# Two-layer cross-attention on one core: last key block padded to 65 rows, first products of the first projection in one piece, result transposes in eights, weights' sums moved

## The chip, the cores and the metric

The kernel runs on one core of one Trainium2 chip. The metric is the device time of one execution in microseconds; lower is better. A core has TensorE (PE in the profile, its weight loads PEld), VectorE (DVE), ScalarE (ACT), GpSimd (POOL) and SyncE (SP), which run side by side and wait for each other at semaphores. Everything is in float32.

## What is computed

Eight batches of 100 query rows (width 1024) attend to 1444 key rows (width 512) twice, with different weights. The first layer adds its projected output to the queries; the second adds its values and normalises. Cut to what matters:

```python
def layer0(query, key, Wq, bq, Wk, bk, Wv, bv, Wo, bo):
    Q, K, V = query @ Wq + bq, key @ Wk + bk, key @ Wv + bv
    weights = softmax(Q @ K.T * 1024 ** -0.5, axis=-1)
    return query + (weights @ V) @ Wo + bo

def layer1(emb, latent, Wq, bq, Wk, bk, Wv, bv, gamma, beta):
    q, k, v = emb @ Wq + bq, latent @ Wk + bk, latent @ Wv + bv
    w = softmax(q @ k.T / sqrt(1024), axis=1)      # over the 100 query rows
    x = w @ v + emb
    return (x - mean(x)) * rsqrt(var(x) + 1e-6) * gamma + beta

x = layer0(x, ctx, ...)       # x: 8 x 100 x 1024, ctx: 8 x 1444 x 512
x = layer1(x, ctx, ...)
```

## The kernel before

**Algebra.** The kernel never builds K or V. It multiplies the weights first (`weight_products`), so that scores are `g @ ctx.T` with g of width 512 per query, and it sums the rows of ctx with the attention weights (`A`, 512 wide) before it projects. Large products are cut in quarters and done with seven products instead of eight, with sums on VectorE (`seven_products`, `inner_product`, `project0`). In these a stationary tile has 128 rows and 128 columns.

**The loop of a batch.** `alternated` runs 48 steps for a batch b: 12 key blocks m times 4 column chunks k. A step gives two matmuls to `weighted_rows` (line 914, the tile A; each has 64 weight columns and goes to one half of the output's partitions) and two to the scores of batch b + 2 (`scores`, line 938, in layer 0; `scores_by_keys`, line 978, in layer 1, the tile s), which also have 64 columns or fewer. In the trace each of these matmuls is two records. In the last two batches of a layer there are no further scores, and A stands alone.

**Rows of A's matmuls.** In layer 0 a key block has 120 rows (124 in the last). In layer 1 a block has 128, and the last has the rest, 1444 - 11 * 128 = 36 (`keys`). The weights of a batch, `w`, have a buffer of 12 blocks of 100 columns, in three rotating buffers; `softmax1` fills the first 36 rows of the last block. `load_rows` brings ctx in four quarters of three blocks, `load_features` its transpose in four chunks; both go through SP's queue into ten rotating buffers (tag "unit"), so that a load is issued when an earlier buffer comes free.

**The first projection.** `project0` (line 1070) is a generator. Its first yield hands out another one, `first`, with eight matmuls of width 400: the products X and Z of one half, for the queries of batches 0 to 3. Its second yield hands out an inner product of seven matmuls of width 200 (tiles o_z_x, o_z_z and so on, called with ahead=True: the sums S1, T1, S3, T3, T2, S2, T4, S4 are given to VectorE first). The caller (lines 1364 to 1379) runs one matmul of `first` after every fourth step of batch 6, and one of the inner product after every fourth step of batch 7; three steps of `queries1`, which give VectorE sums of weights, also go into batch 7. The rest of `project0` follows batch 7.

**The end of a batch in layer 1.** `finish` (line 1271) transposes the 100 finished query rows back with eight matmuls of 100 columns against the identity (line 1249), four for each half, with one step of the loop between the halves. VectorE adds the value bias times the sum of the weights (`r`, line 1253) and forms the statistics; POOL takes the power -1/2, ACT scales, and POOL adds the result to the output by a DMA. The table `finished` says at which step of which batch the seven first batches are finished; batch 7 is finished at the end by `untransposed` and `project_last`.

**The sums of the weights.** `weight_sums` (line 1182, POOL) adds the blocks of `w` to `wsum`, of which there are three buffers. `weight_totals` (line 1198) transposes the wsum of two batches on TensorE and sums them on VectorE to `r`. It is called at step 27 of batches 1, 3 and 5 and at step 8 of batch 7.

**Order.** TensorE's instructions keep the order in which the program gives them (`manual_schedule`). VectorE calls made while `in_order` is set keep theirs; other engines' instructions are placed by the framework's scheduler. PSUM has six banks in the pool "ps" and two in "ps2". After batches 3 and 6 of layer 1 `project1` projects the batches since the last one, and gives VectorE the rest of the softmax of batch 5 or 7 between its products.

## Time and profile before

| what | us |
|---|---|
| median of 3 runs (617.16 to 619.68) | 617.25 |
| profiled execution, its own time | 619.34 |
| its span, first to last instruction | 617.6 |
| PE busy | 604.3 |
| DVE busy | 419.2 |
| ACT busy | 164.8 |
| POOL busy | 100.5 |
| A, 3072 matmul records (line 921), busy | 241.0 |
| s of layer 1, 1472 records (line 990), busy | 116.8 |
| s of layer 0, 1120 records (line 951), busy | 125.5 |
| layer 0, batches 0 to 5 (203.2 to 316.2) | 113.0 |
| layer 0, batches 6 and 7 (316.2 to 345.9) | 29.7 |
| layer 1, batches 0 to 3 (430.8 to 502.4) | 71.6 |
| layer 1, batches 4 and 5 (521.8 to 563.2) | 41.4 |
| layer 1, from batch 7 to the end (586.4 to 617.6) | 31.2 |

The granted clock of TensorE was 0.998 of full speed over the span. Busy times of one engine count overlapping instructions once. The times in brackets are places in the trace, counted from its first instruction; the rows of the loop are read from the first and last records of A. Records of A and s overlap[...]: where both run, one starts 0.043 us after the other in the mean, though each lasts 0.25. So a record's duration says little about its cost, and the distance between starts says it.

### The profile page before, as it was taken

The numbers are of one execution on the slowest core, as the hardware profiler recorded it, in microseconds if no ns is written. First come the engines' busy times: TensorE is split into PE (matmuls) and PEld (weight loads), VectorE is DVE, ScalarE is ACT, GpSimd is POOL, SyncE is SP. The second block draws the span as 40 slices with busy tenths as digits, with TensorE's granted clock in tenths as the row PEclk, the third lists the DMA queues.
The fourth block names the chain that finished last, engine by engine and source line by source line (L and its number), as shares of the span: only waits on it lengthen the run. The fifth ranks groups of instructions, "written<-read, shape, count | busy, mean of one in ns | idle before, by whom it ended". The sixth has DMA issues, their size and how long they took to land.

```text
span 617.6 us, 16433 instructions
## 1 busy us (share of the span) xinstructions
PE 604.3 (98%) x7088; PEld 504.4 (82%) x7088; DVE 419.2 (68%) x915; ACT 164.8 (27%) x374; POOL 100.5 (16%) x141
## 2 busy tenths in 40 slices
PE   9999999999999999998999999999999999999985
PEld 8886467688995999998987666788999999998972
DVE  2986789797793798776559587857423346743785
ACT  1322223314503344323330001103323311134313
POOL 3110111212230000000000001206522202331052
PEclk9999999999999999999999999999999999999999
DMA  8969989746799899999861407955899980796214
GB/s 271 303 140 314 302 229 314 164 99 115 159 287 389 289 345 317 339 323 327 301 213 50 145 0 272 287 183 201 297 338 330 339 305 1 230 342 206 104 29 80
DMA packets 54149, 143.28 MB, mean 232 GB/s; under 512 B 4604, under 2 KB 9980, under 8 KB 54076
## 3 DMA queue, kind: packets, MB, share of 16 engines
q1 hardware_dynamic: 45630, 118.18, 54.4%
q0 software_dynamic: 8048, 23.57, 18.1%
q8 instruction: 56, 0.92, 0.6%
q10 hardware_dynamic: 398, 0.47, 0.2%
q14 instruction: 17, 0.14, 0.1%
HBM read 121.92 MB, written 6.14 MB: 207 GB/s over the span
## 4 chain that ended last, share of the span: by engine, by line
PE 93%; issue 2%; POOL 2%; DMA 1%; ACT 1%; DVE 0%; SPq 0%; POOLq 0%; DVEq 0%
PE A L921 21%; PE s L951 14%; PE s L990 11%; PE qk_x L166 6%; PE g_x L166 5%; PE o_x L166 5%; PE vo_x L166 3%; PE o_y L166 3%; PE g_y L166 3%; PE qk_y L166 2%; PE qk_z L166 2%; PE o_z L166 1%; PE o_w L166 1%; PE qk_w L166 1%; PE vo_z L166 1%
## 5 line engine op out<-in xcount | busy, mean ns | idle before, releaser
L921 PE MATMUL A<-w,c 120*64 120x100 f32 (+2 forms) x3072 | 241.0, 251 | 0.4 <-issue 0.4
L921 PEld LDWEIGHTS A<-w,c 120*64 120x64 f32 (+2 forms) x3072 | 198.7, 136 | 14.2 <-issue 9.5
L951 PE MATMUL s<-cT,g0T 128*64 128x131 f32 (+4 forms) x1120 | 125.5, 286 | 1.6 <-issue 1.5
L990 PE MATMUL s<-g1T,cT 128*64 128x100 f32 (+1 forms) x1472 | 116.8, 251 | 0.0
L990 PEld LDWEIGHTS s<-g1T,cT 128*64 128x64 f32 (+1 forms) x1472 | 96.0, 135 | 4.7 <-issue 1.1
L951 PEld LDWEIGHTS s<-cT,g0T 128*64 128x64 f32 (+2 forms) x1120 | 82.6, 127 | 10.5 <-issue 2.1
L99 DVE STREAM_TRANSPOSE w<-prob 32x384 f32<-32x384 f32 (+1 forms) x128 | 70.7, 553 | 12.5 <-ACT prob L1019 9.8
L1171 ACT ACTIVATE w<-w,negmax 128x100 f32<-128x100 f32 x96 | 35.1, 369 | 69.3 <-DVE negmax L99 69.3
L963 ACT ACTIVATE prob<-s,c 100x394 f32<-100x394 f32 (+3 forms) x32 | 18.0, 564 | 84.4 <-PE s L951 84.2
L99 DVE SCALAR_TENSOR_TENSOR w<-s,kb 128x400 f32<-128x400 f32 (+2 forms) x32 | 13.9, 463 | 33.7 <-PE s L990 33.1
L1414 POOL DMA_DIRECT2D wv<-in_L_xattn_Wv x1 | 0.8, 777 | 188.2 <-PE o_x L166 188.2
L166 PE MATMUL qk_x<-qk 128*128 128x256 f32 x128 | 30.0, 381 | 0.3 <-DMA qk<-in_L_xattn_WkT 0.3
L1012 DVE TENSOR_REDUCE maxima<-prob 100x1 f32<-100x394 f32 (+3 forms) x32 | 16.3, 527 | 19.6 <-ACT prob L963 18.7
L166 PEld LDWEIGHTS qk_x<-qk 128*128 128x128 f32 x128 | 23.2, 190 | 3.6 <-issue 0.7
L1191 POOL TENSOR_TENSOR part<-w 128x500 f32<-128x500 f32 x8 | 10.4, 1296 | 89.9 <-DVE rtotal L99 89.9
L678 ACT ACTIVATE g1T<-g_x,k 128x400 f32<-128x400 f32 x4 | 2.4, 595 | 69.1 <-PE g_x L166 69.0
L1267 ACT ACTIVATE z<-z,rstd 100x1024 f32<-100x1024 f32 x7 | 8.1, 1152 | 44.2 <-POOL rstd L1265 44.1
L99 DVE TENSOR_TENSOR w<-w,rtotal 128x400 f32<-128x400 f32 (+2 forms) x32 | 18.8, 587 | 1.0
L99 DVE TENSOR_TENSOR xT<-xT,o_x 128x400 f32<-128x400 f32 (+1 forms) x32 | 16.0, 541 | 3.6 <-PE o_x L166 3.2
L1171 ACT ACTIVATION_READ_ACCUMULATOR w<-w,negmax 128x1 f32 x96 | 18.3, 190 | 0.0
L1253 DVE SCALAR_TENSOR_TENSOR z<-vectors,r,z 100x512 f32<-100x512 f32 x16 | 11.8, 741 | 8.3 <-PE z L1249 8.0
L1205 DVE TENSOR_REDUCE r<-wsum_ps 100x2 f32<-100x256 f32 x4 | 1.7, 425 | 20.6 <-PE wsum_ps L1203 20.6
(437 smaller groups left out, 1021.2 us busy)
## 6 DMA issues: line engine op xcount, KB each, us to landing
cT<-in_ctxT SPq DMA_DIRECT2D x64, 722.0 KB, 7.5
c<-in_ctx SPq DMA_DIRECT2D x48, 768.0 KB, 6.9
c<-in_ctx SPq DMA_DIRECT2D x16, 512.0 KB, 5.9
vo<-in_L_xattn_Wo SPq DMA_DIRECT2D x8, 512.0 KB, 8.9
qk<-in_L_xattn_WqT SPq DMA_DIRECT2D x8, 512.0 KB
qk<-in_L_xattn_WqT SPq DMA_DIRECT2D x15, 256.0 KB, 5.8
xT<-in_xT SPq DMA_DIRECT2D x2, 1600.0 KB
out<-vectors POOLq DMA_DIRECT2D x7, 400.0 KB, 8.2
```

The costliest lines, as they stand in the source:

```text
L99: ins = getattr(nc.vector, op)(*args, **kw)
L166: nc.tensor.matmul(banks[n // per][:, n % per * width : (n % per + 1) * width], lhs[i][:, n * P : (n + 1) * P], rhs[i], start=(fresh and i ...
L678: nc.scalar.activation(dst[g][:, c, :], banks[j][:, :GT], AF.Identity, bias=u[:, c : c + 1])
L921: nc.tensor.matmul(ps[h * HP : (h + 1) * HP, k * T : (k + 1) * T], c[m // CQ][:r, m % CQ, k * P + h * HP : k * P + (h + 1) * HP], w[:r, m, :],
L951: nc.tensor.matmul(banks[n // per][t[0] : t[1], cuts[n] - o : cuts[n + 1] - o], q[:, k, t0 + t[0] : t0 + t[1]], cT[k][:, cuts[n] : cuts[n ...
L963: nc.scalar.activation(p[:, part], ps[:T, : part.stop - part.start], AF.Identity, bias=key_bias[layer][:T, b : b + 1], scale=SCALE,)
L990: nc.tensor.matmul(banks[m // GM][h * HP : h * HP + n, m % GM * T : (m % GM + 1) * T], cT[k][:, o : o + n], q[:, k, t0 : t0 + T], start=(k ...
L1012: nc.vector.tensor_reduce(maxima[:, n : n + 1], p[:, part], AX.X, ALU.max)
L1171: nc.scalar.activation(rows[:, i, :], rows[:, i, :], AF.Exp, bias=negmax[:, i : i + 1], accum_out=total[:, i : i + 1])
L1191: add(part, w[:, 0:5, :], w[:, 5:10, :], ALU.add)
L1253: nc.vector.scalar_tensor_tensor(z[:, half], bv1[j][:T], s["r"], ps[:T, :], ALU.mult, ALU.add)
L1267: nc.scalar.activation(z, z, AF.Copy, scale=rstd)
```

## The change

The last block of A's products in layer 1 gets 65 rows instead of 36 (`PAD`, `padded`): 29 rows of ctx from the start of the batch fill up its tile, by one more DMA on SP for each batch, and the weights' rows to 64 are set to zero by POOL before softmax1 writes the first 36. The eight products of `first` and the seven of the inner product run in one piece between batches 6 and 7, after the last step of batch 6; the three steps of `queries1` stay at steps 7, 11 and 15 of batch 7. `untransposed` gives its eight transposes without a pause. `weight_totals` runs for the pairs (0, 1) and (2, 3) before the projection after batch 3, for (4, 5) before the one after batch 6, and for (6, 7) at step 28 of batch 7, just before batch 6 is finished; wsum has six buffers.

```diff
--- before.py
+++ after.py
@@ -51,6 +51,7 @@
 LATER = {(1, 5): 4, (1, 7): 4}
 ROWS = [range(0, 4), range(4, 8), range(8, 11), range(11, 12)]
 LAST = (MC - 1) * P
+PAD = HP + 1
 SCALE = 1.0 / math.sqrt(E)
 EPS = 1e-6
 
@@ -887,7 +888,9 @@
                     out=t[:, :n, :], in_=src[r0 : r0 + n * P, :].rearrange("(c p) l -> p c l", p=P)
                 )
                 if n < CQ:
+                    more = PAD - (S - LAST)
                     nc.sync.dma_start(out=t[: S - LAST, n, :], in_=src[LAST:S, :])
+                    nc.sync.dma_start(out=t[S - LAST : PAD, n, :], in_=src[:more, :])
                 yield t
                 continue
 
@@ -910,6 +913,10 @@
     def keys(m):
 
         return P if m < MC - 1 else S - LAST
+
+    def padded(m):
+
+        return max(keys(m), PAD)
 
     def weighted_rows(w, c, dst, name, rows):
 
@@ -999,6 +1006,7 @@
                     yield
         w = weight_rows(f"w{layer}_{b}")
         s["w"] = w[:, : MC * T].rearrange("p (c t) -> p c t", t=T)
+        nc.gpsimd.memset(s["w"][:PAD, MC - 1, :], 0.0)
         s["softmax"] = softmax(s, banks)
         for _ in islice(s["softmax"], LATER.get((layer, b))):
             pass
@@ -1184,7 +1192,7 @@
         b, w = s["b"], s["w"]
         part = work.tile([P, L], F32, tag="half", name=f"part_{b}", bufs=1)[:, : 5 * T]
         part = part.rearrange("p (c t) -> p c t", t=T)
-        wsum = s["wsum"] = work.tile([P, T], F32, tag="wsum", name=f"wsum_{b}", bufs=3)
+        wsum = s["wsum"] = work.tile([P, T], F32, tag="wsum", name=f"wsum_{b}", bufs=6)
         last = MC - 1
         n = keys(last)
         add = nc.gpsimd.tensor_tensor
@@ -1247,11 +1255,8 @@
             ps = bank(f"z_{b}_{j}")
             for e in range(4):
                 nc.tensor.transpose(ps[:T, e * P : (e + 1) * P], xT[:, 4 * j + e, b * T : (b + 1) * T], ident)
-            if j == 0:
-                yield
             half = slice(j * 512, (j + 1) * 512)
             nc.vector.scalar_tensor_tensor(z[:, half], bv1[j][:T], s["r"], ps[:T, :], ALU.mult, ALU.add)
-        yield
 
     def normalise(s):
         b, z = s["b"], s["z"]
@@ -1270,7 +1275,7 @@
 
     def finish(s):
 
-        yield from untransposed(s)
+        untransposed(s)
         normalise(s)
 
     def last_columns(w):
@@ -1346,7 +1351,7 @@
 
         nxt = b + 2 < B
         c, *cT = loaded(load_rows(b, layer), *([load_features(b + 2)] if nxt else []))
-        A = weighted_rows(batches[b]["w"], c, dst, f"A{layer}_{b}", keys if layer else held)
+        A = weighted_rows(batches[b]["w"], c, dst, f"A{layer}_{b}", padded if layer else held)
         some = scores_by_keys if layer else scores
         ahead = some(batches[b + 2], layer, *cT, softmax) if nxt else iter(())
         for _ in range(MC * LC):
@@ -1363,20 +1368,17 @@
     run(steps)
     for b in range(B):
         steps = alternated(b, 0, softmax0, A0[b // G][:, :, b % G * T : (b % G + 1) * T])
+        if b < B - 1:
+            run(steps)
         if b == B - 2:
             o0 = project0(AS, A0)
-        if b < B - 2:
-            run(steps)
-        else:
-
-            more = next(o0)
-            if b == B - 1:
-                gT[1], queries1 = queries(1, wqk1, u1)
+            run(next(o0))
+            run(next(o0))
+        if b == B - 1:
+            gT[1], queries1 = queries(1, wqk1, u1)
             for n, _ in enumerate(steps):
-                if n % 4 == 3 and n > 4:
-                    next(more, None)
-                    if b == B - 1 and n < 16:
-                        next(queries1)
+                if n in (7, 11, 15):
+                    next(queries1)
         for e in range(2 * b, 2 * b + 2) if 2 * b < EC else ():
             add_out_bias(e)
         if b == 0:
@@ -1430,26 +1432,27 @@
     run(first_scores(1, 1, softmax1))
 
     finished = {(4, 2): 0, (4, 16): 1, (4, 30): 2, (5, 34): 3, (7, 2): 4, (7, 15): 5, (7, 28): 6}
-    finishing = []
+    totalled = {3: (0, 2), 6: (4,)}
     for bs in SETS:
         t = wide(f"A1T_{bs[0]}").rearrange("p c t -> p (c t)")[:, : LC * len(bs) * T]
         t = t.rearrange("p (c t) -> p c t", c=LC)
         for i, b in enumerate(bs):
             for n, _ in enumerate(alternated(b, 1, softmax1, t[:, :, i * T : (i + 1) * T])):
-                if b % 2 and n == (8 if b == B - 1 else 27):
-                    weight_totals(batches[b - 1 : b + 1])
                 if (b, n) in finished:
-                    finishing.append(finish(batches[finished[b, n]]))
-                finishing = [f for f in finishing if next(f, finishing) is not finishing]
+                    if (b, n) == (7, 28):
+                        weight_totals(batches[6:8])
+                    finish(batches[finished[b, n]])
             if b == 1:
                 AS = project1_sums(wv1)
         if b == B - 2:
             first = last_columns(wv1)
         if b < B - 1:
 
+            for first_of in totalled[b]:
+                weight_totals(batches[first_of : first_of + 2])
             between, room = {3: (batches[5], (0, 2, 2, 2, 2)), 6: (batches[7], (1, 1, 1, 1, 2))}[b]
             project1(bs, *AS, t, between["softmax"], room)
-    run(untransposed(batches[B - 1]))
+    untransposed(batches[B - 1])
     project_last(batches[B - 1], t, first)
```

## The prediction

> **What bounds the kernel now.** I read the page first: the busy shares and the chain that ended last.

> ```profile
> PE 604.3 (98%) x7088; PEld 504.4 (82%) x7088; DVE 419.2 (68%) x915; ACT 164.8 (27%) x374; POOL 100.5 (16%) x141
> PE 93%; issue 2%; POOL 2%; DMA 1%; ACT 1%; DVE 0%; SPq 0%; POOLq 0%; DVEq 0%
> ```

> TensorE (PE) hardly idles and makes 93% of the chain, so a microsecond of its queue is one of the end, unless another engine then comes late. Busy is not peak: ends of matmuls are modelled. I therefore read when matmuls start, in PE's timeline. First a quiet stretch of layer 1 and a result transpose in it:

> ```profile
> 522.37 0.34 PE L990 MATMUL s<-g1T,cT 128*64 128x100 f32 x4
> 522.54 0.34 PE L921 MATMUL A<-w,c 128*64 128x100 f32 x4
> 522.71 0.34 PE L990 MATMUL s<-g1T,cT 128*64 128x100 f32 x4
> 522.98 0.64 PE L1249 MATMUL z<-ident,xT 128*100 128x128 f32 x4
> 523.55 0.39 PE L921 MATMUL A<-w,c 128*64 128x100 f32 x4
> 523.78 0.34 PE L990 MATMUL s<-g1T,cT 128*64 128x100 f32 x4
> 524.05 0.65 PE L1249 MATMUL z<-ident,xT 128*100 128x128 f32 x4
> ```

> A step (four records of A, four of s, each with 64 weight columns) takes 522.71 - 522.37 = 0.34 us. From one group of transposes (100 columns) to the next is 1.07 us. In it lie four transposes, 0.107 us apart where nothing stands between them, so 0.43, and one step, 0.34: 0.30 us are left for entering and leaving the group. The same with the last key block:

> ```profile
> 446.19 0.39 PE L921 MATMUL A<-w,c 36*64 36x100 f32 x4
> 446.51 0.39 PE L990 MATMUL s<-g1T,cT 128*64 128x100 f32 x4
> 446.83 0.39 PE L921 MATMUL A<-w,c 36*64 36x100 f32 x4
> ```

> A step with 36 rows takes 446.83 - 446.19 = 0.64 instead of 0.34: again 0.30 for a way there and back. And with a 128-column product inside batch 6 of layer 0:

> ```profile
> 318.67 0.91 PE L921 MATMUL A<-w,c 120*64 120x100 f32 x16
> 319.51 0.94 PE L166 MATMUL o_x<-A0T,vo 128*128 128x400 f32 x2
> 320.38 0.91 PE L921 MATMUL A<-w,c 120*64 120x100 f32 x16
> ```

> A period is 1.71 us. Sixteen records of A alone, 0.043 apart, are 0.69; two records of width 400 are 0.67 (eight take 2.69 in the chain): 0.35 for a there and back. None of these is a wait for another engine. PE's only long one is in the list of waits:

> ```profile
> PE wsum_ps L1203 <- POOL wsum L1196: 2.1, 1, 2.1
> ```

> [...] 0.15 us a change; no run here has 65 rows yet. [...]

> **Part 1, 65 rows.** In batches 0 to 5 of layer 1, four A groups of 36 rows alternate with s: 6 x 4 x 0.30 = 7.2 us. In batches 6 and 7 no s stands between; one change of 0.15 goes in each: 0.3. A 120-row and a 128-row matmul of this shape both take 250 ns, so 65 rows cost nothing more. Gain 7.5.
> Added: eight POOL memsets of 65x100 (128x128 took 0.21). Three stand before the wv load, which waits until 372 anyway, and the last of them needs only batch 7 of layer 0, over at 346. The others wait for the end of a batch; behind them on POOL is the sum of the weights, which the trace begins 3.6 us or more after that end, and DVE's first use of the block is 15 us later. Cost 0, if POOL were late up to 0.3 each. Eight SP issues (the present short one takes 0.43), 58 KB each on about 5.9 MB a batch. SP is waiting for buffers in between. The quarter issued at 448.54 is used at 461.3, 12.8 us on; loads land in 6.9 to 7.5 in the median. Cost 0, at worst 8 x 0.2.

> **Part 2, first products in one piece.** Fifteen insertions become one: 14 x 0.35 = 4.9 us less of changes. But the interleaving also hid VectorE. Its timeline:

> ```profile
> 320.78 9.45 DVE L99 STREAM_TRANSPOSE w<-prob 32x384 f32<-32x384 f32 x16 [1.57 <-ACT prob L1019]
> 330.26 1.05 DVE L99 TENSOR_TENSOR xT<-xT,o_x 128x400 f32<-128x400 f32 x2
> 331.23 1.05 DVE L99 TENSOR_TENSOR xT<-xT,o_z 128x400 f32<-128x400 f32 x2
> 332.95 0.57 DVE L934 COPY A0T<-A 128x400 f32<-128x400 f32 x1 [0.67 <-PE A L921]
> 333.44 0.28 DVE L99 TENSOR_TENSOR o_t<-vo 128x128 f32<-128x128 f32 x1
> 333.64 0.36 DVE L99 TENSOR_TENSOR o_t<-A0T 128x200 f32<-128x200 f32 x1
> ```

> The transposes for batch 7 hold DVE until 330.2 whatever PE does, and in the changed program's order of instructions the A0T copy, four additions to xT and then the sums for the inner product (o_z_x and so on) stand behind them. PE: batch 6 starts at 316.24, 48 steps of 0.172 end at 324.5; eight products of 0.67, 330.0; the first two inner products (0.34 each), 330.8. The third needs S1 and T1: 330.26 + 0.49 (copy) + 4 x 0.49 + 0.20 + 0.36 = 333.3. PE idles 2.5 us. Then the fourth waits until DVE has added the first product to xT (six more sums, 334.6 to 334.96) and the last until the fourth's own addition: some 1.4 us more. Batch 7 starts at about 336.5 and ends at 336.6 + 8.26 = 344.9, where the trace has 345.9. Net gain 1.0; bounds -0.5 (each wait half a microsecond longer) and 4.9 (no wait).

> **Part 3, eight transposes together.** One there and back less for each of seven batches: 7 x 0.30 = 2.1. The second bank is free: two of six are needed, three hold scores.

> **Part 4, the sums.** The four groups move next to other 128-column work: 4 x 0.30 = 1.2. The last moves from step 8 to 28 of the last batch, past the 591.9 at which POOL delivers: the 2.1 us wait goes. Their two to four transposes before a projection stay 0.11 us each, as they were; DVE's r (0.42) stands before that projection's sums, which have 2 us of slack or more (DVE waits 0.7 to 1.5 for PE there). Gain 3.3. Six wsum buffers cost room only.

> **The tail.** Of this, PE gains 3.4 after 586.4 (the wait, four groups, half a change). There DVE is next: from 587.1 to 604.8 it is idle only 1.35 and 0.60, so it can come at most 1.95 earlier; 1.10 more lie in its later wait for ol. Sum 3.05: 0.4 of PE's gain is lost.

> **Sum.** 7.5 + 1.0 + 2.1 + 3.3 - 0.4 = 13.5. The profiled execution took 619.34 (span 617.6) and would take 605.8; the median of the runs, 617.25, is 2.1 below it and becomes 603.8. I predict that. A measurement of this kernel tells 0.5%, 3.1 us, from no change.

> **Rivals.**
> - *The waits of part 2 are hidden* (DVE's additions fit between): its whole 4.9, 599.9. Against: DVE's order is fixed. 7%.
> - *PE's clock falls in the gap of part 2.* [...] 607.3. For: 330 to 336.5 has only 2.4 us of products. Against: the longest single gap is 2.5. 8%.
> - *Loads bind layer 1.* Its batches move at 329 to 339 GB/s with DMA 0.93 to 0.94 busy; 5.97 MB in 17.0 us instead of 18.2 asks for 351. If the rate stays, part 1's 7.2 us are lost: 611.0. Against: the lead of about 5 us a load is used up only slowly, 0.6 us a batch. 10%.
> - *Slower: the same loads, but the added 2 KB rows lower the rate.* It decides only once the lead is gone and a batch takes 19.7 us, 303 GB/s: 6 x 2.7 = 16.4 us given back, 620.3 or more. For: 313 GB/s were seen over 277.5 to 298. Against: 1% more bytes. 5%.
> - *The padding leaves the mode as it is* would give 611.3, counted with the loads.

> **How the numbers follow.** Forecast 70% (602 to 606.5 alone, from the bounds of part 2, the tail and the spread of 2.5 us between the runs before). The range takes in the hidden and the clock case: 600 to 608.5, leaving out the loads, slower and half the edges. Faster 0.93 (all but the slower case and a bad end of the loads), same 0.02, slower 0.05.

> **What would show it.** No A group of 36 rows, and the last quarter of a layer-1 batch as fast as the others; a PE wait of 2 to 3 us for DVE's o_t between batches 6 and 7; transposes in eights; no wait of PE for wsum; the tail's DVE nearly without idle time. Waits of PE for c in layer 1, or clock below full at 330 to 340, would make it wrong.

## The result, and the profile after

| us | before | changed |
|---|---|---|
| median of the runs | 618.46 (617.16 to 619.95, 4 runs) | 610.26 (608.37 to 610.98, 4 runs) |
| profiled execution: span, own time | 617.6, 619.34 | 608.7, 610.55 |

The ratio is 0.9862, 95% interval 0.9825 to 0.9899: faster by 1.4%, clear of the noise, but only 8.2 us of the 13.5 that the prediction worked out. (One execution of the experiment without padding, further down, took 1041 us at a granted clock of 0.557; it is left out of its figures.) Of the changed kernel's page, the busy shares:

```profile
PE 591.2 (97%) x7088; PEld 505.0 (83%) x7088; DVE 417.7 (69%) x915; ACT 164.3 (27%) x374; POOL 101.7 (17%) x149
```

PE has 13.1 us less of busy time, about what was predicted, but its share of the span fell: it now idles more. The list of PE's waits says for whom (us in total, times, longest):

```profile
PE A L928 <- issue: 2.4, 2, 1.7
PE o_z_y L167 <- DVE o_t L100: 2.4, 1, 2.4
PE s L997 <- issue: 1.7, 3, 0.8
...
PE o_z_x L167 <- DVE xT L100: 1.0, 1, 1.0
PE z L1257 <- issue: 0.9, 1, 0.9
```

The two waits for DVE were predicted (2.5 and 1.4), and the wait for the weights' sums is gone. The lines with "issue" are the news: PE stands still, and nothing that the profile follows releases it. (The profile before had 1.9 us of such lines, all in layer 0; here all are in layer 1.) The timeline of PE shows the longest of them, in the middle of one loop over one kind of product:

```profile
561.27 1.02 PE L928 MATMUL A<-w,c 128*64 128x100 f32 x20
564.03 1.19 PE L928 MATMUL A<-w,c 128*64 128x100 f32 x23 [1.73 <-issue]
```

The padding does what it says: the last A records have the form 65*64 65x100, and the last quarter of batch 3 takes 4.02 us from its first to its last A record (492.17 to 496.19), as the third does (4.03): no time goes into changes there. No A record has 36 rows, and the transposes stand in eights. To see where the time went, I cut both traces at the first and last A record of each batch (us; the last two columns are experiments further down):

| stage | before | changed | quarters | combined |
|---|---|---|---|---|
| layer 0, batches 0 to 5 | 112.99 | 110.29 | 110.29 | 110.29 |
| layer 0, batch 6 to end of batch 7 | 29.47 | 28.52 | 28.51 | 22.23 |
| from there to layer 1 | 85.12 | 85.13 | 84.77 | 87.25 |
| layer 1, batches 0 to 3 | 71.37 | 68.36 | 66.94 | 66.78 |
| layer 1, batches 4 and 5 | 41.44 | 39.42 | 37.50 | 37.51 |
| layer 1, batch 6 | 8.49 | 10.58 | 8.32 | 8.32 |
| layer 1, batch 7, and the tail | 31.18 | 27.79 | 27.80 | 27.80 |
| the rest | 237.52 | 238.60 | 238.27 | 238.17 |

Layer 1 falls short: batches 0 to 3 gained 3.0 where 5.4 were due (4.8 of part 1, and 0.6 for the two groups of sums that part 4 takes out of them), and batch 6 lost 2.1. The first row is a gain that the change doesn't make: the profile before had three such waits there (0.63, 0.38 and 1.77 us).

**What the waits have in common.** I counted PE's records from the first (weight loads, matmuls, and its sequencer's own, such as waits at semaphores), and set beside each wait the last packet of the queue that the page calls "instruction":

```profile
q8 instruction: 56, 0.92, 0.6%
```

Its columns are packets, MB and the share of 16 engines' time. 56 packets of 16384 bytes for some 14,340 records of PE are 64 bytes a record, 256 records a packet. All seven such steps of the changed kernel (in layer 1), and the three of before (in layer 0):

```
kernel    PE resumes at   step, us   record, modulo 256   after the end of the last q8 packet, us
changed   451.61          0.94       193                  1.49
changed   457.48          0.39       193                  1.40
changed   463.79          0.83       193                  1.41
changed   475.41          0.55       194                  1.43
changed   543.58          1.06       194                  1.41
changed   550.15          1.11       193                  1.39
changed   564.03          1.98       193                  1.54
before    277.13          0.63       194                  1.54
before    283.80          0.38       194                  1.44
before    291.91          1.77       194                  1.61
```

A step here is the time from the start of the matmul before to the start of the one that waited; below, waits of these blocks are counted and summed in the same way, from steps of 0.3 us on. They sum to 6.86 and 2.78 us (a normal step is 0.04). Every one ends at the same place of a block of 256 records, some 1.4 to 1.6 us after a packet of this queue has ended. I read it so: PE waits for its own next block of instructions. The page counts these packets on the same 16 DMA engines as the loads (0.6% of their time, the loads' queue q1 55.8%), and there the engines are nearly full. Their share and GB/s are the last two columns of this table by stretches of layer 1 in the changed kernel (before: 0.92 to 0.95, 329 to 332):

```profile
444.30:462.00 17.70, 16.87 (x380) 16.57 (x377) 5.80 (x17) 4.84 (x26) 3.93 (x8) 1.00 0.99 342
...
479.80:496.50 16.70, 16.70 (x381) 16.59 (x378) 4.82 (x15) 3.82 (x21) 3.97 (x8) 1.00 1.00 353
```

A block lasts PE 256 / 16 steps of 0.342, 5.5 us. The packet itself takes about 1.0 (median of 56: 1.02), and PE goes on 1.4 after its end. An estimate from these, 5.5 - 1.0 - 1.4: it must begin within some 3.1 us after PE entered the block before. Over the eleven blocks that lie wholly in batches 0 to 3 of layer 1, the median packet begins 2.99 us after it in the kernel before and 3.17 in the changed one. So the packets come hardly later than they did: the kernel before was near the edge too (its packets began up to 3.56 us after the entry), but its blocks were longer, 5.5 to 6.8 us, and the shortest time from a packet's end to PE's need was 1.50. In batches 4 to 6 the medians are 2.43 and 3.99. That is still a reading of a trace; what makes the packets late, and whether it costs what it seems to, was for the experiments.

### The profile page after: what moved, and what is told of

It reads as the page before. It is cut to its first block, busy times and chain, and to the rows that moved or that the text cites. A ratio compares the mean times of both kernels' runs of the same rounds, so it can differ in the third digit from the quotient of the medians.

```text
span 608.7 us, 16454 instructions
## 1 busy us (share of the span) xinstructions
PE 591.2 (97%) x7088; PEld 505.0 (83%) x7088; DVE 417.7 (69%) x915; ACT 164.3 (27%) x374; POOL 101.7 (17%) x149
## 3 DMA queue, kind: packets, MB, share of 16 engines
q1 hardware_dynamic: 45870, 118.66, 55.8%
## 4 chain that ended last, share of the span: by engine, by line
PE 91%; DVE 3%; issue 2%; POOL 2%; ACT 1%; DVEq 0%; POOLq 0%; ACTq 0%
PE A L928 19%; PE s L958 13%; PE s L997 11%; PE qk_x L167 7%; PE g_x L167 5%; PE o_x L167 5%; PE vo_x L167 3%; PE o_y L167 3%; PE g_y L167 3%; PE qk_y L167 2%; PE qk_z L167 2%; DVE w L100 2%; PE o_w L167 1%; PE qk_w L167 1%; PE vo_y L167 1%
## 5 line engine op out<-in xcount | busy, mean ns | idle before, releaser
L928 PE MATMUL A<-w,c 120*64 120x100 f32 (+2 forms) x3072 | 229.9, 250 | 2.6 <-issue 2.4
L928 PEld LDWEIGHTS A<-w,c 120*64 120x64 f32 (+2 forms) x3072 | 190.2, 136 | 5.7 <-issue 4.6
L958 PE MATMUL s<-cT,g0T 128*64 128x131 f32 (+4 forms) x1120 | 124.1, 286 | 0.0
L997 PEld LDWEIGHTS s<-g1T,cT 128*64 128x64 f32 (+1 forms) x1472 | 99.7, 135 | 3.9 <-issue 3.3
L958 PEld LDWEIGHTS s<-cT,g0T 128*64 128x64 f32 (+2 forms) x1120 | 69.2, 127 | 8.5 <-PE c L603 0.4
L1009 POOL MEMSET w<- 65x100 f32 x8 | 1.7, 216 | 188.5 <-PE A L928 180.4
L167 PE MATMUL vo_x<-vo 128*128 128x512 f32 x32 | 15.3, 595 | 0.0
```

The lines of the kernel that those rows point to most:

```text
L167: nc.tensor.matmul(banks[n // per][:, n % per * width : (n % per + 1) * width], lhs[i][:, n * P : (n + 1) * P], rhs[i], start=(fresh and i ...
L928: nc.tensor.matmul(ps[h * HP : (h + 1) * HP, k * T : (k + 1) * T], c[m // CQ][:r, m % CQ, k * P + h * HP : k * P + (h + 1) * HP], w[:r, m, :],
L958: nc.tensor.matmul(banks[n // per][t[0] : t[1], cuts[n] - o : cuts[n + 1] - o], q[:, k, t0 + t[0] : t0 + t[1]], cT[k][:, cuts[n] : cuts[n ...
L997: nc.tensor.matmul(banks[m // GM][h * HP : h * HP + n, m % GM * T : (m % GM + 1) * T], cT[k][:, o : o + n], q[:, k, t0 : t0 + T], start=(k ...
```

## Experiments

Each run stands beside runs of the kernel before on the same chip; ratios are to those, with 95% intervals.

### The added rows: one engine, all engines, or nothing

The eight added loads bring eight more 4-byte packets (3426 after 3418), one each, and the last load of the changed kernel ends with some 27 packets of 2 KB one after another, 0.085 us apart, as if all 29 rows went through one engine. So my first theory was one crowded engine. Its rival was that PE's pace alone fills all engines.

68 rows, so that 32 are added:

```diff
-PAD = HP + 1
+PAD = HP + 4
```

> The changed kernel with the last key block padded to 68 rows instead of 65: the added load has 32 rows in place of 29, so 10% more bytes of it, and 32 can be shared evenly by 16 DMA engines, while the trace of the changed kernel ends its loads with some 27 packets of 2 KB one after another, 0.085 us apart, as if one engine had all 29. One-engine theory: PE's unexplained waits in layer 1 (about 7 us in seven places) go, batches 0 to 3 take 66 to 67 us instead of 68.7, the whole 604 to 606 us beside 618.5 of before. Saturation theory (PE asks faster than all 16 engines deliver, wherever the rows lie): waits stay, 609.5 to 611. Theory that PE waits for the keys' data because of the number of loads: no change, 610.

Measured: 612.15 us (607.85 to 613.10), 0.9898 (0.9865 to 0.9930); seven waits, 6.2 us. The trace has 128 more 4-byte packets than that of the kernel before, 16 for each added load where 29 rows brought one: I read it as the rows spread over all 16 engines, and the waits stayed. The one-engine theory falls.

The added loads alone, in the kernel before:

```diff
+PAD = HP + 1
...
+                    more = PAD - (S - LAST)
                     nc.sync.dma_start(out=t[: S - LAST, n, :], in_=src[LAST:S, :])
+                    nc.sync.dma_start(out=t[S - LAST : PAD, n, :], in_=src[:more, :])
```

> The kernel before with nothing but the added loads of 29 rows (eight, 58 KB each); nothing reads those rows. On record: cost 0, at worst 1.6 us. One-engine theory: one engine has 420 KB to move in a layer 1 batch where the mean of all is 367, 19.5 us at the rate of the changed kernel against 18.2 us that PE takes, so PE comes to wait at places 256 instructions apart, and the time rises by 1 to 6 us. Saturation theory: within 1 us of before, since PE asks no faster.

Measured: 617.07 us (616.56 to 620.44), 0.9998 (0.9982 to 1.0014), one such wait in layer 1 (1.07 us, in batch 5), none in batches 0 to 3. Within 0.2% the loads themselves cost nothing, as the prediction said.

The padding alone, in the kernel before (these lines, the memset, and 65-row products):

> The kernel before with the padding to 65 rows alone (loads, memsets, 65-row products). On record: 7.5 us less, 611.0. One-engine theory and saturation theory: 1 to 4 us less, with the repeated waits in layer 1; the first puts what is missing into the loads alone (the run beside this one), the second into PE's higher pace.

Measured: 613.70 us (610.26 to 616.99), 0.9924 (0.9897 to 0.9952), with three waits (1.6 us) in batches 0 to 3. 4.7 us of the 7.5. Since the loads alone brought none of these three, I put them down to the higher pace; the memsets, which run on POOL, were not tried alone. Single waits come at the old pace too: one in layer 1 of the run before this one, three in layer 0 of the kernel before.

The changed kernel without its padding:

> The changed kernel without its padding (36 rows, no added load, no memset); parts 2, 3 and 4 stay. By the sums on record these give 1.0 + 2.1 + 3.3 - 0.4 = 6.0: 612.4 beside 618.5 of before, and no waits in layer 1 that repeat every 256 instructions. One-engine theory: the same 612 to 613, so that the padding as made is worth about 2 us of its 7.5. Saturation theory: 612 to 614, with one or two such waits. If instead parts 2 to 4 are what lost the time: 615 to 617.

Measured: 613.75 us (611.83 to 615.95), 0.9922 (0.9895 to 0.9950), with one wait in layer 1 (0.49). Parts 2 to 4 gave 4.8 of 6.0. The stages show why: the gap between batches 6 and 7 of layer 0 and batch 7 after it took 23.15 us instead of 20.35 in the profile of the changed kernel. In the traces the granted clock changes only at whole multiples of 3.41 us from its first change, wherever the program stands; call these stretches frames. Of each line of the next two views, the number behind the comma is PE's busy time, and the third from the right is the clock. Without padding, one frame holds the wait of 2.40 us and the start of the next one:

```profile
330.24:333.65 3.41, 0.79 (x4) 0.30 (x2) 3.41 (x12) 0.00 (x0) 0.00 (x0) 1.00 0.00 0
333.65:337.06 3.41, 2.59 (x8) 2.50 (x8) 2.31 (x9) 0.00 (x0) 0.00 (x0) 0.50 0.00 0
```

PE was idle for 2.62 of 3.41 us, and the two frames behind it ran at half clock. In the changed kernel's own profile the waits were just as long, 2.40 and 1.04, but the edge of a frame cut them into 1.92 and 1.53, and the clock stayed:

```profile
327.34:330.76 3.42, 1.50 (x7) 0.90 (x5) 3.36 (x9) 0.00 (x0) 0.00 (x0) 1.00 0.00 0
330.76:334.17 3.41, 1.88 (x9) 1.48 (x10) 3.31 (x13) 0.00 (x0) 0.00 (x0) 1.00 0.00 0
```

So the prediction's rival of the clock comes true in some executions: in five of the seven profiled ones with these two waits, for 1.5 us where one frame was lost and 2.5 (68 rows) or 2.8 (here) where two were.

### Bytes or packets

If full engines delay the blocks, it can be the bytes (whatever comes last waits) or what stands ahead in an engine: a row of a feature tile is one packet of 5776 bytes, 221 ns in the trace.

```diff
-            nc.sync.dma_start(out=t, in_=a["ctxT"][b][k * P : (k + 1) * P, :])
+            for h in range(2):
+                part = slice(h * S // 2, (h + 1) * S // 2)
+                nc.sync.dma_start(out=t[:, part], in_=a["ctxT"][b][k * P : (k + 1) * P, part])
```

> The changed kernel with every load of a transposed feature tile (128 rows of 5776 bytes) issued as two, of 2888 bytes a row; the same bytes, more and shorter packets. Theory A (PE's instruction blocks of 16 KB wait in the DMA engines behind a fixed number of packets, so shorter packets let them through): the waits of PE every 256 instructions fall from 5 to 7 us in all to under 3, 605 to 608. Theory B (the engines are full of the loads' bytes, and whatever comes last waits): 609 to 612, waits as before.

Measured: 610.62 us (609.66 to 611.49), 0.9868 (0.9836 to 0.9899). The waits in layer 1 fell from 6.86 us to 4.98 in seven, where theory A expected under 3, and the clock fell in the gap of this profile as well; taken alone it decides nothing. In four pieces:

> The same in four pieces of 1444 bytes a row. Theory A: waits nearly gone, 603.5 to 607. Theory B: 610 or more, since four times as many packets cost the engines something: up to 614.

Measured: 607.45 us (604.52 to 608.61), 0.9814 (0.9778 to 0.9850); half a microsecond above theory A's range. Two waits are left, 0.79 and 0.38 us. The blocks' packets now begin 2.20 us (batches 0 to 3) and 2.24 (4 to 6) after the entry into the block before, in the median; with two pieces it was 2.82 and 3.50, with whole rows 3.17 and 3.99. The engines are as full as ever:

```profile
443.60:461.00 17.40, 17.40 (x398) 17.40 (x395) 6.29 (x19) 5.76 (x32) 4.14 (x9) 1.00 0.99 326
461.00:478.00 17.00, 16.46 (x377) 16.35 (x375) 5.73 (x16) 4.84 (x26) 3.96 (x8) 1.00 0.99 339
```

The reader is to see 0.99 busy and less GB/s than the changed kernel had, and yet PE idle for no more than half a microsecond at a time (in the step of 0.79): the bytes were not the limit. But shorter packets are not all that the edit makes. Of the changed kernel and then of this one, a tile's issue on SP:

```profile
454.21 0.45 SPq L876 DMA_DIRECT2D cT<-in_ctxT  x1
454.24 2.51 SPq L878 DMA_DIRECT2D cT<-in_ctxT  x4
```

A tile is handed to the engines over 1.9 to 4.5 us instead of 0.4 to 1.3; whether the length of the packets or this slower pace lets the blocks through was not separated. The opposite trial takes bytes away and leaves the other packets as they are. The last feature tile of a layer 1 batch is not loaded, and the third is used in its place:

```diff
-    def load_features(b):
+    def load_features(b, layer=0):
...
         for k in range(LC):
+            if layer and k == LC - 1:
+                yield t
+                return
             t = unit(f"cT_{b}_{k}")[:, :S]
```

> The changed kernel with one of the four feature tiles of each layer 1 batch not loaded (the third is used twice), which takes 12% of the bytes of a batch away; every instruction of PE stays. Theories A and B, in both of which full DMA engines delay PE's instruction blocks: the waits go, batches 0 to 3 of layer 1 take 65.6 to 66.5 us instead of 68.4, batch 6 takes 8.3 instead of 10.6, the whole 603 to 606. A theory in which the products with 65 rows or the memsets cost the time: no change, 609 to 611.

Measured: 608.34 us (605.48 to 610.30), 0.9832 (0.9793 to 0.9871). Batch 6 came back to 8.32 us, but batches 0 to 3 stayed at 68.54, and five waits, 3.2 us in all, remained with engines that are no longer full:

```profile
444.30:462.00 17.70, 16.26 (x360) 15.67 (x358) 5.09 (x15) 4.69 (x25) 3.95 (x8) 1.00 0.87 288
```

Both theories missed this. With the run before it, it says that how the loads are cut counts for more than how many bytes they bring: theory B, bytes, falls.

### Blocks of instructions, or places of the program

```diff
-    for _ in range(8):
+    for _ in range(40):
         nc.tensor.matmul(warm[:, :P], ones, ones, start=True, stop=True)
```

> The changed kernel with 32 more matmuls in the loop that warms TensorE up at the start: 64 more instructions of PE (a weight load and a matmul each) before everything else. In all traces so far the waits end at the 193rd or 194th of 256 records of PE, counted from the first. If they belong to blocks of 256 instructions, they stay at 193 or 194 of the new count, that is 64 instructions (1.4 us) earlier in the program. If they belonged to places of the program (data that comes late there), they would be found at 1 or 2 of 256. Time: 610 and at most 4 us more for the added matmuls.

Measured: the six waits end at records 194, 194, 193, 194, 194 and 194 of 256 (450.64, 456.99, 474.32, 486.21, 492.46 and 555.41 us), though all of the program had moved by 64. They belong to blocks of instructions. The time was 615.51 us (613.00 to 616.54), 0.9942 (0.9886 to 0.9999): the added matmuls cost 5.9 us before the first A, more than I allowed.

### The gap of part 2

The inner product goes behind batch 7; the eight first products stay in the gap:

```diff
             run(next(o0))
-            run(next(o0))
...
+    run(next(o0))
     next(o0)
     next(queries1)
     run(o0)
```

> The changed kernel with the inner product (o_z) taken out of the gap between batches 6 and 7 of layer 0 and put after batch 7; the eight first products stay in the gap. If VectorE's order is what PE waits for there, as on record: no waits of 2.4 and 1.0 us in the gap, which shrinks from 12.1 to 5.6 us, with full clock in batch 7; 4.7 us of products come after it, with 0 to 1.4 us of waits: 606 to 608 in all, and less spread than the changed kernel, since the clock's fall in some executions (23.2 us instead of 20.4 for gap and batch 7) goes too. If VectorE is as late after batch 7: 609.5 to 611.

Measured: 606.94 us (606.27 to 608.35), 0.9816 (0.9789 to 0.9844). The gap took 7.22 us instead of 12.14, where 5.6 was expected: 1.4 of it is a new wait of batch 7, at 328.31. The profile calls it "issue"; DVE ends the transposes of that batch's weights at 328.21, so I take it for a wait for them. From batch 7 to layer 1 there are 4.3 us more. With the waits of layer 1 still there (6.5 us), these stages gained 0.6 in the profiles, and by the ratios the whole gained 2.8. That fits a clock that no longer falls: the mean clock of its four executions is 0.996 to 0.997, that of the changed kernel's 0.993 to 0.996.

### Both mends

Four pieces, and the sums of the inner product made ahead of batch 7, where DVE is idle:

```diff
             run(next(o0))
-            run(next(o0))
         if b == B - 1:
+            inner_z = next(o0)
...
+    run(inner_z)
     next(o0)
```

> The changed kernel with both mends: feature tiles loaded in four pieces of 1444 bytes a row, and the inner product (o_z) after batch 7, with its sums on VectorE issued before that batch, where VectorE is idle for 6 us. If the two losses are separate they add: no waits every 256 instructions (under 0.8 us in all), the gap between batches 6 and 7 at 7.2 us, clock at full in batch 7, and 85.1 + 4.7 us from batch 7 to layer 1 without the waits of 0.4 and 1.0: 601.5 to 604.5. If the pieces only helped by chance in the runs of quarters: 605 to 608.

Measured: 600.57 us (599.79 to 600.95), 0.971 (0.969 to 0.973): better than both kernels, and than expected. Not only the two mends add up: with the sums made ahead, the gap, batch 7 and the way to layer 1 take 3.6 us less than in the run before this one (22.23 + 87.25 instead of 23.60 + 89.46). Its waits, all that the list has:

```profile
PE warm L112 <- DVE ones L109: 1.1, 1, 1.1
PE A L930 <- issue: 0.5, 2, 0.3
```

and the gap, with no wait left in it:

```profile
322.10 2.95 PE L167 MATMUL o_x<-A0T,vo 128*128 128x400 f32 x8
324.89 2.85 PE L167 MATMUL o_z<-A0T,vo 128*128 128x400 f32 x8
327.77 1.47 PE L930 MATMUL A<-w,c 120*64 120x100 f32 x29
```

The pieces alone in the kernel before:

> The kernel before with the feature tiles in four pieces, nothing else. Theory A: its own waits every 256 instructions, all in layer 0 (0.6, 0.4 and 1.8 us in its profile), go: 0.5 to 2.5 us less, and the fall of the clock behind the wait for the weights' sums stays. If the pieces shorten the loads in general, layer 1 becomes faster too, by more than 1 us: it should not, by theory A.

Measured: 618.20 us (615.59 to 619.60), 0.9987 (0.9977 to 0.9997). The waits of layer 0 are gone (110.29 instead of 112.99 us), which says little, as other profiles with whole rows had none there either. Layer 1's batches 0 to 3 are unchanged (71.36), as theory A has it; but batch 7 of layer 1 took 17.03 us instead of 15.51. There the clock fell behind the wait of 2.1 us for the weights' sums. Two frames of the kernel before, then two of this run:

```profile
588.00:591.41 3.41, 1.86 (x27) 1.36 (x25) 2.94 (x5) 0.00 (x0) 3.03 (x6) 1.00 0.00 0
591.41:594.83 3.42, 2.90 (x41) 2.34 (x41) 2.43 (x5) 0.09 (x1) 1.93 (x3) 1.00 0.03 5
```

```profile
587.10:590.51 3.41, 1.32 (x22) 1.01 (x22) 1.95 (x6) 0.00 (x0) 1.97 (x6) 1.00 0.00 0
590.51:593.92 3.41, 3.41 (x28) 2.46 (x24) 2.08 (x3) 1.15 (x1) 1.71 (x2) 0.50 0.02 5
```

The same wait lies across two frames before, and within one here. The two runs with only the loads or only the padding had the fall too (17.02 and 16.82 us). All cases together, by PE's idle time in the frame that has most of it:

```
waits                        idle in one frame, us                        next frame
part 2, in the gap           no padding 2.62, 68 rows 2.40, halves 2.39,  half clock
                             fewer loads 2.47, 64 records more 2.84
part 2, in the gap           changed 1.92, quarters 1.86                  full
for the weights' sums        loads alone 2.08, padding alone 2.05,        half clock
                             before with quarters 2.09
for the weights' sums        before 1.56                                  full
```

In all traces, after the first 20 us, every frame with 2.05 us or more of idle time was followed by half clock, and no frame with 1.84 or less was, unless the clock was at half already; between these, in the run with eight pieces below, 1.85 and 1.95 were followed by half clock, and another 1.95 was not. The falls also hide what the pieces gain in the kernel before: 18 of its 22 executions with pieces have a mean clock under 0.996, and 14 of 27 without. At like clock the pieces save 2.1 us (means of 615.95 and 618.03 where it is higher) and 0.8 (618.23 and 619.06 where it is lower), as theory A expected.

Eight pieces, in the combined kernel:

> The combined kernel with eight pieces of some 722 bytes instead of four. Theory A asks only that packets be short enough: no better than the combined kernel (within 0.7 us). If the engines pay a fixed price for each packet, twice as many packets take more of their time, loads come late and it is slower by 2 us or more; if more pieces still gain, waits were left in the combined one.

Measured: 657.75 us (654.79 to 661.93), 1.0644 (1.0611 to 1.0677). PE waits for data:

```profile
PE s L960 <- DMA cT<-in_ctxT: 22.5, 17, 2.4
PE A L930 <- DMA c<-in_ctx: 11.3, 9, 2.6
```

A packet of 720 bytes took 35 ns, no more than its share of the 62 ns for 1444, and the engines were 0.64 to 0.86 busy: they were not the limit. SP issued a piece every 0.48 us, 3.8 us for a tile, which can't be used before its eighth piece. How much of the loss that order of issue explains was not tried.

## Why the prediction was wrong

It said 603.8, within 600 to 608.5, and it is 610.3. By its own steps:

- **What bounds the kernel**: right, PE's queue; PE's busy time fell by 13.1 us.
- **Part 1, 7.5**: the price of a change between 36-row and other products (the prediction's change of mode, 0.15 us) was right. That 65 rows need none was not shown by any trace of before; the 4.02 us above show it. With four pieces, batches 0 to 3 took 4.43 us less than before where 5.4 were due, and two waits of 1.2 us in all were still in them; batch 6 took 0.17 less where 0.15 were due. What failed is the sentence that gave the loads' lead ("12.8 us on; loads land in 6.9 to 7.5") as the reason why a faster PE would find all it needs. It looked at the data alone. PE's instructions come by DMA packets as well, each begun about 3 us after PE entered the block before (medians 2.99 before, 3.17 after), and part 1 shortened the block: from an average of 5.5 x 71.37 / 66.94, 5.9 us, to 5.5. A term for PE's wait for its own instructions was missing. Measured: 6.9 us of such waits in layer 1 of the profiled execution, none there before. The cost of the added loads, 0, was right.
- **Part 2, net 1.0**: 0.95 in the profile; the waits 2.4 and 1.0 instead of 2.5 and 1.4. But in other executions the clock takes 1.5 to 2.8 us more, the case to which 8% was given, at a price of 3.5. By the mean clock it looks like the usual case: traces with a fall have 0.991 to 0.995 (eight pieces apart), traces without 0.996 to 0.998, and the three executions of the changed kernel that have no trace here have 0.993, 0.995 and 0.993. How their times divide between the clock and the instruction waits is not known. The prediction set against this case that its longest single gap is 2.5 us; that such a gap is too short was not shown by any trace. Here about 2 us of idle time (1.85 at the least) were enough if they fell into one frame of 3.41, in one wait or two. The frames do not begin at one place in all executions: the first change of the clock came at 4.32 us in the profile before and at 6.49 in that of the changed kernel. An estimate from the lengths of the waits, with frames that may begin anywhere and a limit of 1.85 to 2.05: the two waits of part 2 meet it in 92 to 81% of executions, the one wait for the sums in 53 to 41%.
- **Part 3, 2.1, and part 4, 3.3, less 0.4**: batch 7 and the tail took 3.4 us less where 3.05 were due. Batches 4 and 5 with four pieces took 3.94 less; part 1's share of that is 2.4, parts 3 and 4 have the rest (four groups of transposes, 1.2, and one of sums, 0.3, were due). What it didn't see: the wait that part 4 removes also cost the clock 1.3 to 1.5 us in some executions of the kernel before.
- **The sum**: 13.5, less 6.9 of new waits, plus the 2.8 of before's own, is 9.4; the two profiled executions differ by 8.8. The remainder, 0.6, lies in small steps (0.65 before the first A).
- **The rivals**: "Loads bind layer 1" gave 611.0, nearly the result, with a mechanism that falls: it said that the rate of 329 to 339 GB/s would stay. The changed kernel moved 342 to 353, and with four pieces 324 to 339 sufficed for nearly the full gain. That it came near the result is luck.

That PE waits for blocks of instructions is shown by the shift of 64 records, and that the way in which the loads are issued makes the blocks late, by the four pieces, at the same busy share of the engines. Whether the length of the packets or the slower issue does it was not separated, and how an engine chooses between its queues is not shown.

## What to carry to other kernels

Before a kernel whose bound engine runs through hundreds of instructions in a few microseconds is made faster, look at "issue" waits and at the queue called "instruction": count the records between two waits, and if it is 256, as here, try the loads beside it in pieces before making them fewer. Pieces have a lower limit too: four of 1444 bytes gave the changed kernel 0.5% here, and eight of some 722 instead of four made the combined kernel 57 us slower. And two or three microseconds of waits on TensorE cost another 1.3 to 2.8 in clock here, in executions in which enough of them fell into one frame. So compare a profile's clock with those of the other executions before one profile is taken for all, and fill such a gap even where the sum says it is paid for.
